# A decoder layer's feed-forward part split into two passes, with a seven-product down projection

## The chip, the cores and the metric

The kernel runs on one core of a Trainium2 chip. TensorE multiplies, VectorE (DVE in the profile) and ScalarE (ACT) do the element-wise work, GpSimd (POOL) does sums over partitions, and nearly all transfers are issued from the queue of SyncE (SP). Times are device microseconds of a whole execution; before and after are compared by the median of several runs. In the profile "PE" is a matmul, "PEld" the load of its stationary operand, and L88 means line 88 of the kernel.

## The reference

The layer takes x, 8 sequences of 100 tokens of width 1024, and a context. It applies a retention-like attention, a cross attention to the context, and a gated feed-forward part, each followed by a residual sum and a normalization without weights. Only the last of the three changes here:

```python
gate = jnp.einsum('bsd,hd->bsh', x, w_gate)      # 4096 x 1024
up = jnp.einsum('bsd,hd->bsh', x, w_up)          # 4096 x 1024
gated = jax.nn.silu(gate) * up
y = jnp.einsum('bsh,dh->bsd', gated, w_down)     # 1024 x 4096
x = _layernorm(x + y, axis=-1)
```

## The kernel before

Everything lies with the model's width on the 128 partitions and tokens along the free dimension. The 800 tokens are two halves of N = 400. The width 1024 is KT = 8 blocks of 128, or two groups of QT = 4. A float32 product is made from three faster ones: each operand is split into a rounded high part and a remainder (`split`, `split2`: a ScalarE cast, L69, and a VectorE subtraction, L70), and `mm3` (L87 to L90) issues high x high, high x low and low x high into one PSUM bank. So one 128 x 128 x 400 block costs three matmuls of 400 columns.

The feed-forward part begins at L761. Its input, the normalized result of the cross attention, is kept as four block operands: b11 and b21 are the upper and lower 512 rows of the first half of the tokens, b12 and b22 those of the second. The hidden width 4096 is 32 blocks of 128, taken in 16 units (`UNITS`) of two.

Gate and up of unit 0 are made directly (L871 to L879): 2 x 2 x 2 products of 8 blocks. For the other 15 units, the function `seven` (L831) treats two hidden blocks x two token halves as a 2 x 2 block matrix product and makes it with 7 block products in place of 8. A block product is `prod`: 4 blocks of contraction x 3 matmuls, 12 matmuls into a bank of its own (`next_bank`). Their sums are made afterwards on VectorE, in the helpers `copied` (ScalarE, L849) and `add` (L853). Mixed weights come from `w_pair` (L814), mixed inputs from `mix_all` (L795), which runs while the direct products of unit 0 and the first products of unit 1 do.

The down projection is not made by seven products. `hidden` (L894) multiplies silu(gate) by up, splits the result and leaves it in on-chip tiles `hd`. Whenever two units are ready (three at the very end), `down` (L911) loads their down weights, and `into_y2` (L905) makes each of the 8 output blocks x 2 token halves and adds it to the on-chip sum `y2`, which starts as the residual. So gate, up and down alternate. The last three units are made over 500 and then 300 tokens (`CUT`); the normalization of the 500 runs under the matmuls of the 300, and that of the 300 (`norm_root`, `scaled`) is the tail.

A second form of the seven-product scheme stands in the first attention: `wino` (L334) with `in_turn` (L390). It keeps three banks per unit and lets TensorE itself add up products in one of them (`start=False`), so that only three VectorE additions and three ScalarE copies are left. `in_turn` interleaves two neighbouring units: one unit's last three products alternate with the first three of the next.

What order instructions have on each engine is settled when the program is built: a scheduler places them by program order (earlier or `high_priority` code first) and by its own model of when each is ready, and gives tiles of a pool their buffers, `bufs` of them to a tag. On the chip each queue then runs strictly in that order. The SP queue in particular holds every load and store: an instruction at its head that waits for a buffer holds back all later transfers.

Raw weights arrive in three buffers `wst` of 512 KB, split weights lie in four buffers `w`, and the `big` pool has four tiles of 1.6 MB.

Of the kernel before, what the change touches and what calls it, by code (L numbers as in the profile page):

```python
# [16 lines left out]
P = 128  # L17
# [17 lines left out]
LAST = 3  # L35
CUT = 5 * T
# [5 lines left out]
def decoder_layer(ctx, tc, xT, cT, w1, wo1, w2, wo2, wc, w3, wd, gw, qw, kw, trig, dec, mask, out):  # L42
# [118 lines left out]
    wcd = dr.tile([2 * NKV, P, 2, KT * P], FR, name="wcd")  # L161

    bigpool = sbuf("big", 2 * KT // QT)
    bp = bigpool.__enter__()
# [159 lines left out]
    def load_raw(src):  # L324
        st = wp.tile([P, KT * P], F32, tag="wst", name="wst", bufs=3)
        nc.sync.dma_start(out=st, in_=src)
        return st
# [6 lines left out]
    def wino(pool, src0, src1, zb, temp, tags):  # L334
# [12 lines left out]
        def copied(acc):  # L347
            t = temp()
            with tc.high_priority():
                nc.scalar.copy(t, acc)  # L350
            return t

        def add(t, acc):
            with tc.high_priority():
                nc.vector.tensor_tensor(t, acc, t, ALU.add)
            return t
# [9 lines left out]
        p1 = copied(x)  # L366
# [4 lines left out]
        c11 = add(p1, z)  # L371
# [3 lines left out]
        u2 = copied(x)  # L375
        yield
        prod(y, (tb, 0), "t3")
        p7 = copied(y)
# [3 lines left out]
        c22 = add(p7, x)  # L382
        yield
        prod(y, (tb, 1), "t4", start=False)
        c21 = add(u2, y)
        yield
        prod(x, (tv, 1), "b22", start=False)
        return c11, x, c21, c22

    def in_turn(units):  # L390

        at = sorted((7 * i + 2 * j, i) for i in range(len(units)) for j in range(-1, 7))
        started = {}
        for _, i in at:
            make, then = units[i]
            if i not in started:
                started[i] = make()
            try:
                next(started[i])
            except StopIteration as e:  # L400
                then(e.value)


    with sbuf("l1", 2) as p:
# [118 lines left out]
        def after_qk(h):  # L523
            def then(c):
                c11, c12, c21, c22 = c
                for (half, i), acc in zip(HB, (c11, c22, c21, c12)):
                    of_qk(half, i, acc)
            return then

        def after_v(h):  # L530
            def then(c):
                c11, c12, c21, c22 = c
                for (half, blk), acc in zip(HB, (c11, c22, c21, c12)):
                    of_v(half, blk, acc, acc is c12)
                core(h)
            return then

        def after_g(h):
            def then(c):
                c11, c12, c21, c22 = c  # L540
                gated(h, {(half, blk): silu(acc, None if acc is c12 else acc)
                          for (half, blk), acc in zip(HB, (c11, c22, c21, c12))})
            return then

        in_turn([(lambda h=h, i=i: wino(p, w1[h, i], w1[h, i + 1], zb, temp, "ass"), then(h))
                 for h in range(1, NH1) for i, then in ((0, after_qk), (2, after_v), (4, after_g))])
# [213 lines left out]

    fp = ctx.enter_context(sbuf("fp", 1, "right"))  # L761
    z2pool = sbuf("z2", 1, "right")
    z2p = z2pool.__enter__()
    zb, ys = {}, []

    def z_tile(name):
        return z2p.tile([P, 2, QT, N], FR, tag=name, name=name)

    def temp(bufs=8):
        return fp.tile([P, N], F32, tag="s", name="s", bufs=bufs)  # L770

    zz = fp.tile([P, 2, 2, QT, N], FR, tag="y2", name="zz")

    def make_z2(half):
        if half == 0:
            return [z_tile("b11"), zz[:, 0]]
        return [zz[:, 1], z_tile("b22")]

    def mix(dst, pairs):
        for j, (a, b, op) in enumerate(pairs):  # L780
            if not isinstance(a, bass.AP):
                rs = y2p.tile([P, N], F32, tag="rs", name="rs", bufs=2)
                nc.sync.dma_start(out=rs, in_=zd2[0, :, a])
                a = rs
            t = y2p.tile([P, N], F32, tag="mix", name="mix")
            nc.vector.tensor_tensor(t, a, b, op)
            split(dst[:, :, j], t)

    def after2(half, y):
        ys.append(y)  # L790
        if half == 0:
            zb["b21-b11"] = z_tile("b21-b11")
            mix(zb["b21-b11"], [(y[:, QT + j], y[:, j], ALU.subtract) for j in range(QT)])

    def mix_all(y):  # L795
        js = range(QT)
        for name, pairs in (("b11+b22", [(j, y[:, QT + j], ALU.add) for j in js]),
                            ("b12-b22", [(y[:, j], y[:, QT + j], ALU.subtract) for j in js]),
                            ("b21+b22", [(QT + j, y[:, QT + j], ALU.add) for j in js]),
                            ("b11+b12", [(j, y[:, j], ALU.add) for j in js])):  # L800
            zb[name] = big([P, 2, QT, N])
            mix(zb[name], pairs)
# [3 lines left out]
    zb["b11"], zb["b22"] = z2[0][0], z2[1][1]  # L806

    ring = [0]

    def next_bank():  # L810
        ring[0] += 1
        return bank("aaassssv"[ring[0] % 8])[:, :N]

    def w_pair(*ops):  # L814

        w = wp.tile([P, 2, KT * P], FR, tag="w", name="w", bufs=4)
        for c, (x, y, op, keep) in enumerate(ops):
            t = x
            if y is not None:
                t = fp.tile([P, H], F32, tag="as", name="as") if keep else x  # L820
                nc.vector.tensor_tensor(t, x, y, op)
            e = slice(c * H, (c + 1) * H)
            split2(w[:, 0, e], w[:, 1, e], t)
        return w

    def first_pair(i, part, r1=None):
        r1 = load_raw(w3[i + 1, part]) if r1 is None else r1
        a21, a22 = r1[:, :H], r1[:, H:]
        return w_pair((a21, a22, ALU.add, True), (a22, None, None, True))

    def seven(i, part, t0=None):  # L831

        r0, r1 = load_raw(w3[i, part]), load_raw(w3[i + 1, part])
        a11, a12, a21, a22 = r0[:, :H], r0[:, H:], r1[:, :H], r1[:, H:]
        t0 = first_pair(i, part, r1) if t0 is None else t0
        t1 = w_pair((a11, a22, ALU.add, True), (a11, None, None, True))
        t2 = w_pair((a12, a22, ALU.subtract, True), (a21, a11, ALU.subtract, False))
        t3 = w_pair((a11, a12, ALU.add, False))

        def prod(w, c, z):  # L840
            acc = next_bank()
            for k in range(QT):
                e = slice(c * H + k * P, c * H + (k + 1) * P)
                mm3(acc, w[:, 0, e], w[:, 1, e], zb[z][:, 0, k], zb[z][:, 1, k], k == 0, k == QT - 1)
            return acc

        def copied(acc):
            t = temp()
            nc.scalar.copy(t, acc)  # L849
            return t  # L850

        def add(t, x, y, op=ALU.add):
            nc.vector.tensor_tensor(t, x, y, op)  # L853

        s2 = copied(prod(t0, 0, "b11"))
        s4 = copied(prod(t0, 1, "b21-b11"))
        add(s2, s2, s4)
        s1 = copied(prod(t1, 0, "b11+b22"))
        add(s1, s1, s4)
        add(s4, s1, s2, ALU.subtract)  # L860
        s3 = copied(prod(t1, 1, "b12-b22"))
        add(s4, s4, s3)
        add(s1, s1, prod(t2, 0, "b21+b22"))
        add(s4, s4, prod(t2, 1, "b11+b12"))
        m5 = prod(t3, 0, "b22")
        add(s1, s1, m5, ALU.subtract)
        add(s3, s3, m5)
        return s1, s3, s2, s4


    ws = [[load_w(w3[i, part]) for part in range(2)] for i in range(2)]  # L871
    gs = []
    for half in range(2):
        for i in range(2):
# [4 lines left out]
            gs.append(t)  # L879
    t0s = [first_pair(2, part) for part in range(2)]  # L880
    mix_all(ys[1])
    y2pool.__exit__(None, None, None)

    with sbuf("ff", 1) as p:
        def new_hid():
            return [p.tile([P, 2, 2 * N], FR, tag="hd", name="hd", bufs=4) for _ in range(2)]

        def gate(i, t0=None):
            g = seven(i, 0, t0)
            for t in g:  # L890
                nc.scalar.activation(t, t, AF.Silu)
            return g

        def hidden(i, g, t0=None, make=new_hid):  # L894
            u = seven(i, 1, t0)
            hid = make()
            for n, (a, b) in enumerate(zip(g, u)):
                nc.vector.tensor_tensor(a, a, b, ALU.mult)
                split(hid[n // 2][:, :, n % 2 * N:(n % 2 + 1) * N], a)
            return hid  # L900

        def load_wd(u, mq, w=None):
            return load_w(wd[u, mq], w)

        def into_y2(ws, hid, m, a, e):  # L905
            acc = bank(acc_tag())[:, :e - a]
            for k, h in enumerate(hid):
                mmw(acc, ws[k // 2], m % QT * 2 + k % 2, h[:, 0, a:e], h[:, 1, a:e], k == 0, k == len(hid) - 1)
# [120 lines left out]
```

## Time and profile before

| what | value |
| --- | --- |
| median of 3 runs (lowest to highest) | 2551.64 us (2550.22 to 2552.69) |
| the profiled execution's own time | 2551.76 us |
| its span, first to last instruction | 2550.0 us |
| matmul instructions recorded | 14186 |
| transfers | 353.93 MB, mean 139 GB/s |

The profiled execution lies within the spread of the timed runs. The page gives busy times of each engine over the span, then 40 slices of 63.75 us each; the feed-forward part begins a little after 1735 us and takes slices 28 to 40. A row of a stretch of time gives for each engine its busy us and its instruction count, then the clock that TensorE was granted (1.00 is full speed), the mean busy share of the 16 DMA engines and the rate. A row of a group of instructions gives line, engine, operation, output and inputs, shape, count, busy us, mean ns of one, then the idle time just before them and what ended it.

### The profile page before, as it was taken

To read this page: it belongs to the slowest core of one execution; us is meant where nothing else is said; L and a number is where in the kernel's file an instruction comes from. 1 tells how busy PE (TensorE), PEld (TensorE's weight loads), DVE (VectorE), ACT (ScalarE), POOL (GpSimd) and SP (SyncE) were. 2 spreads that over 40 slices of the span, in tenths; PEclk is the share of its full clock that TensorE was granted. 3 is DMA by queue.
4 is the path that set the end of the run, shared out by engine and by line. 5 is a ranking of instruction groups with operands and counts; after the bars stand their busy time and mean duration, and the time that the engine had idled before them with its cause. 6 is when DMAs were issued, how large, how long until landed. Compare 5 with 4: busy or idle time off the path is not lost.

```text
span 2550.0 us, 37518 instructions
## 1 busy us (share of the span) xinstructions
PE 2504.3 (98%) x14186; PEld 2462.7 (97%) x14186; DVE 2006.9 (79%) x3316; ACT 1338.8 (53%) x2390; POOL 471.7 (18%) x230
## 2 busy tenths in 40 slices
PE   8999999998999999999999999999999999999997
PEld 8999999998899999999999999999999999999996
DVE  7778876569999788898998998767875865865886
ACT  6676676336777466565565565434432433432351
POOL 0111111002555243333343343100000000000000
PEclk9999999999999999999999999999999999999999
DMA  7333445764444555455455455474412211211221
GB/s 237 109 113 122 142 142 197 246 248 151 140 141 166 185 185 167 132 180 161 145 176 161 150 185 187 139 263 132 141 50 67 83 50 67 83 50 67 67 75 52
DMA packets 165940, 353.93 MB, mean 139 GB/s; under 512 B 45530, under 2 KB 108378, under 8 KB 156542
## 3 DMA queue, kind: packets, MB, share of 16 engines
q1 hardware_dynamic: 164606, 347.33, 40.9%
q0 software_dynamic: 1152, 4.19, 1.1%
q8 instruction: 111, 1.82, 0.3%
q14 instruction: 71, 0.58, 0.1%
HBM read 283.09 MB, written 68.39 MB: 138 GB/s over the span
## 4 chain that ended last, share of the span: by engine, by line
PE 87%; DVE 7%; DMA 2%; issue 2%; ACT 1%; SPq 0%; DVEq 0%; ACTq 0%
PE a L90 16%; PE a L88 16%; PE a L89 16%; PE s L89 10%; PE s L90 10%; PE s L88 10%; PE v L88 3%; PE v L90 2%; PE v L89 2%; DVE r L122 1%; PE s L473 1%; PE s L668 1%; DVE r L121 1%; DVE d L70 1%; DVE w L70 1%
## 5 line engine op out<-in xcount | busy, mean ns | idle before, releaser
L88 PE MATMUL a<-big,w 128*128 128x400 f32 (+2 forms) x1796 | 606.0, 338 | 9.7 <-ACT big L69 6.4
L89 PE MATMUL a<-big,w 128*128 128x400 f32 (+2 forms) x1796 | 606.1, 338 | 0.0
L90 PE MATMUL a<-big,w 128*128 128x400 f32 (+2 forms) x1796 | 604.3, 337 | 0.0
L69 ACT CAST w<-wst 128x1024 fp32r<-128x1024 f32 (+2 forms) x292 | 251.4, 864 | 260.4 <-PE a L90 112.0
L70 DVE TENSOR_TENSOR w<-wst,w 128x1024 fp32r<-128x1024 f32 (+2 forms) x292 | 290.7, 998 | 104.6 <-ACT w L69 103.3
L88 PEld LDWEIGHTS a<-big,w 128*128 128x128 f32 x1796 | 338.4, 188 | 10.9 <-ACT big L69 7.0
L89 PEld LDWEIGHTS a<-big,w 128*128 128x128 f32 x1796 | 338.7, 189 | 1.6 <-DVE big L70 0.6
L90 PEld LDWEIGHTS a<-big,w 128*128 128x128 f32 x1796 | 338.7, 189 | 0.7
L127 POOL PARTITION_ALL_REDUCE ss<-sq x56 | 161.2, 2885 | 332.7 <-DMA zd<-y 166.6
L88 PE MATMUL s<-big,w 128*128 128x400 f32 x596 | 207.9, 350 | 2.4 <-ACT big L69 2.4
L89 PE MATMUL s<-big,w 128*128 128x400 f32 x596 | 206.8, 347 | 1.7 <-DVE big L70 1.7
L90 PE MATMUL s<-big,w 128*128 128x400 f32 x596 | 206.3, 347 | 0.0
L591 POOL PARTITION_ALL_REDUCE kss<-ksq x64 | 165.5, 2586 | 140.8 <-ACT ksq L590 140.1
L69 ACT CAST w<-as 128x512 fp32r<-128x512 f32 x90 | 55.9, 621 | 214.2 <-PE a L90 180.1
L702 ACT ACTIVATE s<-s,rk 128x400 f32<-128x400 f32 x160 | 88.2, 592 | 95.1 <-DVE sm L724 64.5
L127 POOL PARTITION_ALL_REDUCE mb<-sm x32 | 83.4, 2607 | 217.5 <-DVE sm L724 217.5
L853 DVE TENSOR_TENSOR s<-s 128x400 f32<-128x400 f32 x183 | 102.3, 568 | 24.9 <-ACT s L849 19.2
L721 ACT ACTIVATE s<-s 128x800 f32<-128x800 f32 (+1 forms) x128 | 95.3, 749 | 45.6 <-DVE s L715 42.2
L88 PEld LDWEIGHTS s<-big,w 128*128 128x128 f32 x596 | 112.6, 189 | 4.5 <-ACT big L69 3.6
L89 PEld LDWEIGHTS s<-big,w 128*128 128x128 f32 x596 | 112.5, 189 | 3.2 <-DVE big L70 2.3
L90 PEld LDWEIGHTS s<-big,w 128*128 128x128 f32 x596 | 113.0, 190 | 0.0
L70 DVE TENSOR_TENSOR pl<-s,ph 128x800 fp32r<-128x800 f32 (+1 forms) x128 | 108.2, 850 | 1.1 <-ACT ph L69 1.0
(315 smaller groups left out, 6222.6 us busy)
## 6 DMA issues: line engine op xcount, KB each, us to landing
wst<-in_w SPq DMA_DIRECT2D x137, 512.0 KB
w<-wcd SPq DMA_DIRECT2D x64, 1024.0 KB
wst<-in_wo SPq DMA_DIRECT2D x64, 512.0 KB
wst<-in_wd SPq DMA_DIRECT2D x32, 512.0 KB
big<-o1d SPq DMA_DIRECT2D x16, 800.0 KB
qd<-d SPq DMA_DIRECT2D x32, 400.0 KB
q<-qd SPq DMA_DIRECT2D x32, 400.0 KB
o2d<-oh SPq DMA_DIRECT2D x32, 400.0 KB
```

The lines of the kernel that those rows point to most:

```text
L69: nc.scalar.copy(hi, src)
L70: nc.vector.tensor_tensor(lo, src, f32(hi), ALU.subtract)
L88: nc.tensor.matmul(acc, lh, rh, start=start, stop=False, skip_group_check=chain)
L89: nc.tensor.matmul(acc, lh, rl, start=False, stop=False, skip_group_check=chain)
L90: nc.tensor.matmul(acc, ll, rh, start=False, stop=stop, skip_group_check=chain)
L121: nc.vector.scalar_tensor_tensor(q, ss, eps, q, ALU.add, ALU.mult)
L122: nc.vector.scalar_tensor_tensor(q, q, 3.0, r, ALU.subtract, ALU.mult)
L127: nc.gpsimd.partition_all_reduce(y, x, P, op)
L591: nc.gpsimd.partition_all_reduce(ss[:, at], sq[:, at], P, RED.add)
L702: nc.scalar.activation(sc, sp, AF.Copy, scale=rk[:, c:c + 1])
L721: nc.scalar.activation(e, e, AF.Exp)
L853: nc.vector.tensor_tensor(t, x, y, op)
```

## The change

Three parts. First, `wino` becomes the common helper `seven` (raw weights may come as two strided slices; a result is passed to a callback `got`, or added to an existing tile `into`), and the old `seven`, `w_pair`, `first_pair`, `next_bank` and `mix_all` go. Gate and up of units 1 to 15 use the new helper under `in_turn`; the mixed inputs t1 to t4 are made in `after2`, ahead of unit 0's direct products.

Second, gate and up are finished for all units before the down projection begins. `gated_block` multiplies, and `combine` writes each unit's hidden blocks to DRAM: for the first twelve units in the seven forms that the scheme needs as its right operand (`hd`, by quarters of four units, 7 chunks of 1.6 MB to a quarter), for the last four as they are (`h3d`).

Third, the down projection runs as a second pass: for three quarters of the hidden width, `down_unit` makes two output blocks x two token halves by seven block products, added into `y2`; the fourth quarter is made by plain products, half by half of 400 tokens, followed by the normalization. Chunks are loaded one quarter ahead into buffers that the first pass has left (`slots`).

```diff
-    def wino(pool, src0, src1, zb, temp, tags):
+    def seven(pool, src0, src1, zb, tags, temp=None, got=None, into=None):
...
-        def copied(acc):
-            t = temp()
+        def first(acc, name):
             with tc.high_priority():
+                if into is not None:
+                    nc.vector.tensor_tensor(into[name], acc, into[name], ALU.add)
+                    return None
+                t = temp()
                 nc.scalar.copy(t, acc)
...
+        def put(name, j, a, b):
+            t = y2p.tile([P, N], F32, tag="mix", name="mix", bufs=3)
+            nc.vector.tensor_tensor(t, a, b, ALU.subtract)
+            split(zb[name][:, :, j], t)
+            return t
+        for j in range(QT):
+            r = []
+            for k in (j, QT + j):
+                r.append(y2p.tile([P, N], F32, tag="rs", name="rs", bufs=2))
+                nc.sync.dma_start(out=r[-1], in_=zd2[0, :, k])
+            t2 = put("t2", j, y[:, QT + j], put("t1", j, y[:, j], r[0]))
+            put("t3", j, y[:, QT + j], y[:, j])
+            put("t4", j, r[1], t2)
...
+    def gated_block(u, name, acc):
+        if u not in hid:
+            hid[u] = ff.tile([P, 4, N], F32, tag="r", name="r")
+        r = hid[u]
+        at = r[:, C.index(name)]
...
+            nc.vector.tensor_tensor(at, acc, gates[u, name], ALU.mult)
+        done[u] = done.get(u, 0) + 1
+        if done[u] == 4:
+            combine(u, r)
+    def combine(u, r):
+        h = ff.tile([P, 7, N], FR, tag="h", name="h")
+        q, j = u // QT, u % QT
+        if q == QT - 1:
+            split2(h[:, 0:4], r, r)
...
+            return
+        t = ff.tile([P, 4, N], F32, tag="t", name="t")
+        pairs = r.rearrange("p (i x) n -> p i x n", x=2)
+        nc.vector.tensor_tensor(t[:, 0:2], pairs[:, :, 1], r[:, 0:2], ALU.subtract)
+        nc.vector.tensor_tensor(t[:, 2], r[:, 3], t[:, 0], ALU.subtract)
+        nc.vector.tensor_tensor(t[:, 3], r[:, 2], t[:, 2], ALU.subtract)
+        split2(h[:, 3:7], t, t)
+        split2(h[:, 1:3], r[:, 2:4], r[:, 2:4])
+        split2(h[:, 0], r[:, 0], r[:, 0])
+        to = lambda a, b, l: f32(hd[q, a:b, :, l, j]).rearrange("c p n -> p c n")
+        nc.sync.dma_start(out=to(0, 7, 0), in_=f32(h))
+        nc.sync.dma_start(out=to(0, 1, 1), in_=r[:, 0:1])
+        nc.sync.dma_start(out=to(1, 3, 1), in_=r[:, 2:4])
+        nc.sync.dma_start(out=to(3, 7, 1), in_=t)
...
+    def after_up(u):
+        if u == QT:
+            load_chunk(0, down_order[:1])
+        elif u == UNITS - 2:
+            load_y(fp)
+        elif u == UNITS - 1:
...
+            load_y(ctx.enter_context(sbuf("yy", 1)))
+            slots[0:0] = [lambda: hk.tile([P, 2, QT, N], FR, tag="h", name="h", bufs=2)] * 2
+    slots = [f_tile, z_tile, z_tile] + [lambda: big([P, 2, QT, N])] * 4 + [z_tile]
+    down_order = ("b11", "b21", "t2", "t3", "t1", "t4", "b22")
...
+    def load_chunk(q, names):
+        for name in names:
+            chunk[q, name] = next_slot()
+            nc.sync.dma_start(out=f32(chunk[q, name]), in_=f32(hd[q, ORDER7.index(name)]))
...
+    def down_unit(q, m):
+        def make():
+            if m == 0 and q == 0:
+                load_chunk(0, down_order[1:])
+            z = {name: chunk[q, name] for name in ORDER7}
+            into = {"c%d%d" % (i + 1, j + 1): y2[m // 2][:, i, j * N:(j + 1) * N] for i in range(2) for j in range(2)}
+            return seven(fp, down_w(q, m), down_w(q, m + 1), z, "ass", into=into)
+        def then():
+            if m != 2:
+                return
+            if q < QT - 2:
+                load_chunk(q + 1, down_order)
+            else:
+                for half in range(2):
+                    z3.append([next_slot() for _ in range(2)])
+                    for i in range(2):
+                        nc.sync.dma_start(out=f32(z3[half][i]), in_=f32(h3d[2 * i + half]))
+        return make, then
...
+    in_turn([unit(u) for u in range(1, UNITS) for unit in (gate_unit, up_unit)]
+            + [down_unit(q, m) for q in range(QT - 1) for m in range(0, KT, 2)])
...
-            for a, e in ((0, CUT), (CUT, 2 * N)):
...
+            y = rows(half)
+            s1 = lnp.tile([P, N], F32, tag="s1", name="s1", bufs=2)
+            for m in range(KT):
+                acc = proj(w_split(load_raw(down_w(QT - 1, m))), z3[half], tag=acc_tag())
+                nc.vector.tensor_tensor(y[:, m], y[:, m], acc, ALU.add)
+                add_up(s1, y, m)
+            r = norm_root(y, s1, lnp, idle_pe=half == 1)
+            scaled(y, r, lambda m, half=half: out[:, m, half * N:(half + 1) * N])
```

`down_w` slices the down weights so that each transfer moves runs of 128 values (512 bytes).

## The prediction

> **What bounds the kernel now.** First the busy shares, then TensorE's waits, then stretches of the feed-forward part.
>
> ```profile
> span 2550.0 us, 37518 instructions
> PE 2504.3 (98%) x14186; PEld 2462.7 (97%) x14186; DVE 2006.9 (79%) x3316; ACT 1338.8 (53%) x2390; POOL 471.7 (18%) x230
> PE a L88 <- ACT big L69: 6.4, 1, 6.4
> 100.00:400.00 300.00, 299.81 (x1802) 297.73 (x1801) 230.05 (x339) 207.83 (x330) 38.18 (x18) 1.00 0.41 130
> 1664.00:1684.00 20.00, 18.72 (x99) 18.09 (x99) 13.65 (x21) 8.01 (x12) 0.00 (x0) 1.00 1.03 404
> 1735.00:1818.00 83.00, 78.33 (x399) 75.02 (x400) 65.39 (x119) 38.78 (x72) 0.00 (x0) 0.96 0.45 147
> 1800.00:1850.00 50.00, 45.93 (x233) 44.13 (x232) 39.47 (x71) 21.46 (x40) 0.00 (x0) 0.93 0.32 101
> 1850.00:2450.00 600.00, 600.00 (x3294) 599.92 (x3293) 427.96 (x739) 216.75 (x403) 0.00 (x0) 1.00 0.20 65
> 2530.40:2550.00 19.60, 6.70 (x20) 2.77 (x19) 14.22 (x30) 7.68 (x16) 0.00 (x0) 0.82 0.47 168
> ```
>
> TensorE is the bound, and from 1850 to 2450 it never pauses at full clock: 3294 matmuls in 600 us are 182.2 ns each, the price of a 400-column matmul here. DVE has room (71%), transfers far more (65 GB/s; 1664 to 1684 shows that 404 can be had, all DMA engines busy). The losses of the feed-forward part lie at its ends. From 1735 to 1818, 399 matmuls ran where 83 / 0.1822 = 456 fit: 57 x 0.182 = 10 us lost, of which the largest single wait of the whole list, 6.4 us for a `big` tile (a mixed input), is one. After the last product at 2530.4 come 19.6 us of normalization. The first attention (100 to 400 us) runs `wino` and `in_turn` already: TensorE gapless there with DVE at 230 / 300 = 77%.
>
> **Matmuls removed.** Direct products of unit 0 and the seven-product gate and up stay: 192 + 15 x 2 x 84 matmuls. Down before: 32 hidden blocks x 8 output blocks x 2 halves x 3 = 1536. After: three quarters x 4 units x 84 = 1008, and the last quarter 8 x 8 x 2 x 3 = 384; together 1392. So 144 fewer; at 182.2 ns from the 1850 to 2450 row **-26.2 us**. The 500- and 300-column split goes too, but it counted the same columns, so it adds nothing. All of it is on the path, since TensorE has no pause to hide it in. This is the firm term.
>
> **Does anything else become the bound in pass one?** The unit of work is gate plus up, 168 x 0.1822 = 30.6 us of TensorE. The DVE rows of the two forms:
>
> ```profile
> L70 DVE TENSOR_TENSOR w<-wst,w 128x1024 fp32r<-128x1024 f32 x48 | 58.5, 1220 | 45.2 <-ACT w L69 45.2
> L355 DVE TENSOR_TENSOR tp<-s,tp 128x400 f32<-128x400 f32 x33 | 18.8, 569 | 13.8 <-PE s L90 11.6 <-ACT w L69 2.1
> L363 DVE TENSOR_TENSOR ws<-wst 128x512 f32<-128x512 f32 x16 | 11.0, 689 | 0.3
> L853 DVE TENSOR_TENSOR s<-s 128x400 f32<-128x400 f32 x117 | 65.6, 568 | 13.0 <-ACT s L849 9.8 <-PE s L90 2.8
> L821 DVE TENSOR_TENSOR as<-wst 128x512 f32<-128x512 f32 x62 | 42.5, 685 | 26.1 <-DMA wst<-in_w 26.1
> ```
>
> The old `seven` took 9 additions x 0.568 + 5 weight sums x 0.685 + 7 remainders x 0.685 = 13.3 us of DVE. The new takes 4 x 0.69 + 3 x 1.22 + 0.69 + 3 x 0.569 = 8.8. Two of them, 4 products silu(gate) x up (2.3) and `combine` (1600 elements of differences and 2800 of remainders, eleven times the 400-column 0.569, less the overhead saved on wide ones: an estimate of 5.4 us) make 25.3 us of 30.6: 83%, somewhat above the 77% that left TensorE gapless. ACT needs about 14. So pass one should stay TensorE-bound: **0**, up to +15 if it doesn't (third rival). `combine` also stores 2.87 MB a unit; with 2.1 MB of weights 163 GB/s against 404. It hides.
>
> **Start of the feed-forward part.** `mix_all` and `b21-b11` mixed 20 tiles, `after2` mixes 16, and weight sums of the first unit shrink. The old wait arose because mixing was put behind the next units' weights. Now mixing stands ahead. From the end of the normalized rows (1765 us in DVE's order of time) DVE has 8 remainders of z (8 x 0.49, back to back), 14 mixes until t2 is whole (14 x 0.98), first unit's weights 5.9 and odd ends 1.5: ready near 1790, less up to 4 us of weight work that fits the pauses before. TensorE wants t2 after the direct products and two block products, near 1782 + 4.4 = 1787. So a wait of 0 to 4 us where 10 were lost: -10 to +5 against now, taken as **-4**.
>
> **The junction of the passes.** Here the new cost lies. `load_chunk` needs the buffers of z and `big` that the last up unit is still reading, so six chunks (6 x 1.64 = 9.8 MB) can only be fetched as that unit's products release them. With the weights of two or three down units (2.1 to 3.1), the stores of units 14 and 15 (3.3) and y2 (3.3), 18.5 to 19.5 MB want to move within 19 block products, 19 x 12 x 0.1822 = 41.5 us. At the measured 404 GB/s that takes 46 to 48 us, 5 to 7 late; part of it (unit 15's store, half of y2) isn't needed at once, which takes off up to 8 us of traffic. The Trainium skill's "DMA: Bandwidth & Descriptors", Bandwidth, speaks against the change more: for traffic between HBM and on-chip memory it gives a limit of about 358 GB/s per core. By it the junction would be 10 to 13 us late. The trace of this kernel shows 404 for 20 us, so I go by the row: 0 to 7, taken as **+5**; by the page's figure it would be +11. A wait of that length costs more than itself: the 1800 to 1850 stretch, after the 6.4 us wait, shows a mean clock of 0.93. The skill's "TensorE: Matmul & The Clock Gate" (Part 1) puts this at half clock after an idle window of about 3.4 us; 7% of 50 us is 3.5 us, which I let stand in the +5 and in the wide side of the range.
>
> **Pass two.** A down unit takes 84 x 0.1822 = 15.3 us; DVE 7.1 + 7 additions x 0.569 = 11.1 (73%), now for every bank, since `first` with `into` leaves ScalarE. A quarter (61 us) loads 11.5 MB of chunks and 4.2 of weights, 257 GB/s of 404. The weights come in 512-byte runs, which the trace doesn't show; packets under 2 KB are most of its packets all the same. Bounds: nothing, or half the weights' rate (+13 us of transfers a quarter, still under 61). Chunks are asked for ten products before they are used, 22 us. The price is what `then` puts on SP ahead of the next weights: three chunks with free buffers, 4.9 MB, 12 us, against about five products (11 us) for which three `wst` buffers let weights run ahead. **+2** over three boundaries, 0 to 30 (second rival).
>
> **The tail.** 400 columns for 300: eight subtractions (+0.8), sixteen variance matmuls (5.2 us in the tail, +1.1), the chain of roots (+0.5), the scaling (+0.8), the last store (+0.3); less 0.7, since the other part's scaling no longer sits between, as its half is done under the last 192 matmuls (35 us, DVE some 31 of them). **+2.5**, 0 to +5.
>
> **Sum** against the profiled execution's own 2551.8: -26.2 - 4 + 5 + 2 + 2.5 = -20.7, so 2531.1. That execution is 0.1 us above the median of the runs, so the same figure stands for the median: **2531 us**.
>
> **Rivals.** First, *the junction hides and the start loses nothing*: -26.2 - 9 + 2.5 gives 2519. For it: 404 GB/s, and old chunks known long before; against it: the six buffers come free only one by one. Chance 0.16.
>
> Second, *weights queue behind chunks on SP*, the case slower than before. At the junction and the two quarter boundaries after it, SP's one queue carries chunk transfers ahead of weights. Four chunks are 16.2 us at 404 GB/s, a unit's weights 2.6, their split 1.05 + 1.22; 21 us against a lead of 11 leaves TensorE idle for 10, three times, 30 us more: 2561. It decides from (2551.8 - 2531.1) / 3 = 7 us a boundary. For it: a queue in strict order, and `load_chunk` ahead of a unit's weights in the program; against it: the scheduler places a load only when its model has the buffer free, and 257 of 404 GB/s is no saturation on the mean. Chance 0.11.
>
> Third, *pass one becomes bound by DVE*: the tile `r` is single, so the next unit's first product of silu(gate) and up waits until `combine` has been stored. From the last block product of a unit to that one lie 4 products, 8.7 us; multiply, differences, cast, remainder and a 1.43 MB store (3.5 us at 404, plus its latency) need about 12. DVE then stands at a wait for some 3 us of its 5 spare a unit. If 1.3 us of each reaches TensorE, 15 x 1.3 = 20 us are lost: 2551, no change. Chance 0.08.
>
> **How the numbers follow.** The main course has 0.65; its own range is 2523 to 2543 (junction +11, start +1, or both small). Its gain alone is firm, its stalls are not. The range 2517 to 2555 takes in the first rival but its edge, the third, and part of the second. The measurement tells 0.2%, 5.1 us, from no change. Faster: 0.65 + 0.16 + a third of the third rival = 0.84; same 0.05; slower 0.11.
>
> **What would show it.** Right: 14042 matmuls or so; rows of pass one and of pass two at full clock with 5.49 matmuls a us, DVE near 80% and 70%; a DMA share near 1 for some 40 us at the junction, and TensorE's waits there on chunk loads or weights, 2 to 10 us in all; the wait for `big` at the start under 5 us; a tail near 22 us. Wrong: waits for `wst` or `w` at each quarter boundary, or DVE waits for stores of `r` that reach TensorE, or a pass one under 5.4 matmuls a us.

## The result and the profile after

| | before | after |
| --- | --- | --- |
| median of 5 runs each, us | 2552.58 (2550.22 to 2555.21) | 2527.52 (2526.38 to 2527.76) |
| the profiled execution's own time / its span, us | 2551.76 / 2550.0 | 2527.58 / 2525.8 |
| feed-forward part: first matmul to last product, us from the span's start | 1735.1 to 2530.3 | 1735.7 to 2504.6 |
| matmuls recorded | 14186 | 14042 |
| transfers, MB | 353.93 | 438.16 |

The ratio is 0.9901 with a 95% interval of 0.9887 to 0.9916: faster by 1%. By the two profiled spans it is 24.2 us. The prediction said 2531 us, 20.7 us less than before. The total is near; three of its terms (the start, the junction and pass two) are not, and they partly cancel.

First the head of the page after: its span, TensorE's row (busy us, share, count), and the row of the DMA engines' busy tenths in 40 slices of 63 us.

```profile
span 2525.8 us, 37215 instructions
PE 2478.2 (98%) x14042; PEld 2440.9 (97%) x14042; DVE 2000.6 (79%) x3106; ACT 1353.7 (54%) x2272; POOL 466.8 (18%) x230
...
DMA  7333445774444654455554554575455445388742
```

TensorE lost 26.1 us of busy time. The slices 3, 8, 8, 7 near the end (2147 to 2400 us) are the place where one pass gives way to the other.

Now the stretches of the feed-forward part after. The columns are from:to, length, busy us and count of PE, PEld, DVE, ACT, POOL, the granted clock, the DMA engines' busy share, GB/s.

```profile
1735.70:1818.00 82.30, 82.25 (x443) 80.88 (x444) 73.48 (x126) 42.82 (x72) 0.00 (x0) 1.00 0.43 137
1818.00:2220.00 402.00, 402.00 (x2208) 402.00 (x2207) 312.54 (x413) 194.34 (x271) 0.00 (x0) 1.00 0.47 161
2220.00:2260.00 40.00, 40.00 (x222) 40.00 (x221) 28.15 (x38) 14.08 (x19) 0.00 (x0) 1.00 1.00 372
2260.00:2300.00 40.00, 38.95 (x209) 37.41 (x208) 23.97 (x35) 8.20 (x9) 0.00 (x0) 1.00 0.91 322
2300.00:2350.00 50.00, 46.50 (x246) 45.63 (x245) 33.93 (x50) 11.44 (x13) 0.00 (x0) 0.97 0.67 239
2350.00:2500.00 150.00, 150.00 (x821) 149.41 (x821) 93.55 (x136) 41.31 (x47) 0.00 (x0) 1.00 0.51 169
2504.60:2525.80 21.20, 7.40 (x19) 2.75 (x18) 10.27 (x20) 6.43 (x12) 0.00 (x0) 0.79 0.21 77
```

Read it by counts: 5.49 matmuls a us is a TensorE that never pauses. The first stretch has 443 of 452 that fit; before, 399 of 456. Pass one, 1818 to 2220, is without a gap. The junction (2220 to 2260) has the DMA engines full and no pause at all. The next two stretches are where time goes: 209 of 219.5, and 246 of 274.5. After 2350 it is dense again to the end of the products.

Adding up how much later than 0.182 us after its predecessor each matmul starts (excesses under 0.05 us left out), within those stretches, gives the ledger that the rest of this text uses. Such a sum is good to some 0.2 us.

| term | us | how read |
| --- | --- | --- |
| 144 matmuls fewer | -26.2 | 14186 - 14042, at 182.2 ns |
| start of the feed-forward part | -8.7 | pauses and slow matmuls: 10.5 before, 1.8 after |
| junction | 0 | 222 matmuls in 40 us |
| pass two | +7.8 | two stalls, about 2291 and 2328 |
| slow matmuls in the last quarter | +0.9 | at 2473 and 2494, beside the first half's normalization |
| tail | +1.5 | 19.7 to 21.2 |
| part ahead, not changed | +0.7 | starts at 1735.1 and 1735.7 |
| sum | -24.0 | spans: -24.2 |

The second stall is the larger one, 5.6 us. SyncE's queue in order of time (start, us from the first issue's start to the last one's end, what, how many; `wst` are down weights, the rest chunks of later quarters), then what DVE, ScalarE and TensorE did; a bracket is the idle time before an instruction and what ended it, and no bracket means that it followed at once. L364 adds a product to the sum `y`, L370 is the first sum made of the new weights.

```profile
2302.81 0.34 SPq L911 DMA_DIRECT2D z<-hd  x1
2305.36 2.51 SPq L911 DMA_DIRECT2D big<-hd  x2
2308.05 8.02 SPq L327 DMA_DIRECT2D wst<-in_wd  x4
2316.16 2.37 SPq L911 DMA_DIRECT2D big<-hd  x1
```

```profile
2320.77 0.57 DVE L364 TENSOR_TENSOR y<-s,y 128x400 f32<-128x400 f32 x1 [0.52 <-PE s L88]
2322.96 0.58 DVE L364 TENSOR_TENSOR y<-s,y 128x400 f32<-128x400 f32 x1 [1.62 <-PE s L88]
2325.15 0.57 DVE L364 TENSOR_TENSOR y<-a,y 128x400 f32<-128x400 f32 x1 [1.61 <-PE a L88]
2325.64 0.68 DVE L370 TENSOR_TENSOR ws<-wst 128x512 f32<-128x512 f32 x1
```

```profile
2327.20 1.99 ACT L67 CAST w<-wst 128x1024 fp32r<-128x1024 f32 x2 [18.18 <-DVE wst L371]
```

```profile
2328.30 0.45 PE L86 MATMUL s<-f,w 128*128 128x400 f32 x1 [3.19 <-ACT w L67]
...
2329.75 0.54 PE L87 MATMUL a<-h,w 128*128 128x400 f32 x1
```

And the DMA engines' busy tenths from 2300 to 2330, in 40 slices of 0.75 us:

```profile
DMA  9997988999999999999999989999999992000000
```

Three chunk loads, 4.9 MB, were issued just ahead of the four pieces of down weights that TensorE needs next; the two to `big` are for the third quarter, which TensorE reaches some 50 us later. The issuing of the four pieces took 8.0 us, where a single one at 2299.7 took 0.43. The last thing that keeps the engines full, until 2325, is the chunk asked for at 2316.2.

But the weights were not late for all of the time until 2325.6. The semaphores in the trace show the two pieces that L370 needs landed at 2319.6 and 2320.5, 12 us after they were asked for, and the other two by 2322.1. L370 began 5.2 us after the second of its pieces was there, and its row has no idle time before it: it stood in VectorE's own order behind three additions, each of which waited for a product of TensorE. From L370's start to the waiting matmul's start takes 2.7 us; begun at 2320.5 it would, by an estimate from these figures, have let that matmul go at 2323.2, and TensorE's pause began at 2325.1. So what held TensorE last was VectorE's order, which is settled when the program is built. At the first stall it was the same: the weights had landed at 2286.2, and the additions kept their first sum until 2290.9.

ScalarE had been idle 18.2 us; TensorE stood 3.2 us for the cast, and then ran a few us at half speed (matmuls of 0.54 us for 0.34).

### The profile page after: what moved, and what is told of

It is laid out like the page before. It is cut to its first block, busy times and chain, and to the rows that moved or that the text cites. A ratio compares the mean times of both kernels' runs of the same rounds, so it can differ in the third digit from the quotient of the medians.

```text
span 2525.8 us, 37215 instructions
## 1 busy us (share of the span) xinstructions
PE 2478.2 (98%) x14042; PEld 2440.9 (97%) x14042; DVE 2000.6 (79%) x3106; ACT 1353.7 (54%) x2272; POOL 466.8 (18%) x230
## 2 busy tenths in 40 slices
DMA packets 232898, 438.16 MB, mean 173 GB/s; under 512 B 47594, under 2 KB 176490, under 8 KB 220302
## 4 chain that ended last, share of the span: by engine, by line
PE 89%; DVE 6%; issue 2%; DMA 1%; ACT 1%; SPq 0%; DVEq 0%; ACTq 0%
PE a L88 18%; PE a L86 18%; PE a L87 17%; PE s L88 9%; PE s L87 9%; PE s L86 9%; PE v L86 2%; PE v L88 2%; PE v L87 2%; PE s L486 1%; PE s L677 1%; DVE r L120 1%; DVE r L119 1%; PE s L148 1%; DVE d L68 1%
## 5 line engine op out<-in xcount | busy, mean ns | idle before, releaser
L86 PE MATMUL a<-big,w 128*128 128x400 f32 (+2 forms) x1824 | 616.3, 339 | 10.5 <-ACT big L67 7.1
L87 PE MATMUL a<-big,w 128*128 128x400 f32 (+2 forms) x1824 | 615.7, 338 | 0.0
L88 PE MATMUL a<-big,w 128*128 128x400 f32 (+2 forms) x1824 | 614.4, 338 | 0.0
L67 ACT CAST w<-wst 128x1024 fp32r<-128x1024 f32 (+1 forms) x243 | 251.8, 1039 | 431.0 <-PE s L88 152.3
L68 DVE TENSOR_TENSOR w<-wst,w 128x1024 fp32r<-128x1024 f32 (+1 forms) x243 | 297.7, 1227 | 120.2 <-ACT w L67 119.0
L86 PEld LDWEIGHTS a<-big,w 128*128 128x128 f32 x1824 | 343.7, 189 | 12.3 <-ACT big L67 7.4
L87 PEld LDWEIGHTS a<-big,w 128*128 128x128 f32 x1824 | 344.5, 189 | 1.4 <-DVE big L68 0.3
L88 PEld LDWEIGHTS a<-big,w 128*128 128x128 f32 x1824 | 344.2, 189 | 1.0 <-DVE w L68 0.3
L86 PE MATMUL s<-big,w 128*128 128x400 f32 x680 | 236.0, 347 | 0.1
L87 PE MATMUL s<-big,w 128*128 128x400 f32 x680 | 234.7, 345 | 0.0
L88 PE MATMUL s<-big,w 128*128 128x400 f32 x680 | 234.6, 346 | 0.0
L86 PE MATMUL a<-z,w 128*128 128x400 f32 x504 | 174.5, 346 | 8.2 <-ACT r L118 4.3
L88 PE MATMUL a<-z,w 128*128 128x400 f32 x504 | 174.9, 347 | 0.7 <-DVE w L68 0.7
L87 PE MATMUL a<-z,w 128*128 128x400 f32 x504 | 175.0, 347 | 0.0
L87 PE MATMUL s<-z,w 128*128 128x400 f32 x416 | 144.5, 347 | 2.3 <-DVE z L68 2.3
L86 PE MATMUL s<-z,w 128*128 128x400 f32 x416 | 145.2, 349 | 0.0
L88 PE MATMUL s<-z,w 128*128 128x400 f32 x416 | 145.1, 349 | 0.0
L86 PEld LDWEIGHTS s<-big,w 128*128 128x128 f32 x680 | 127.6, 188 | 1.4 <-ACT w L67 0.4
L87 PEld LDWEIGHTS s<-big,w 128*128 128x128 f32 x680 | 127.6, 188 | 1.1
```

The lines of the kernel that those rows point to most:

```text
L67: nc.scalar.copy(hi, src)
L68: nc.vector.tensor_tensor(lo, src, f32(hi), ALU.subtract)
L86: nc.tensor.matmul(acc, lh, rh, start=start, stop=False, skip_group_check=chain)
L87: nc.tensor.matmul(acc, lh, rl, start=False, stop=False, skip_group_check=chain)
L88: nc.tensor.matmul(acc, ll, rh, start=False, stop=stop, skip_group_check=chain)
```

## Experiments

Three batches of kernels, each compared with the kernel before on the same chip; times are medians.

### How much is the count of matmuls worth?

All four quarters of the down projection are made by plain products again, from h3d; two passes, gate and up by the new helper and everything ahead are kept. The first form fetched three of the first quarter's four chunks only when the first pass had ended:

```diff
-    hd = dr.tile([QT - 1, 7, P, 2, QT, N], FR, name="hd")
-    h3d = dr.tile([4, P, 2, QT, N], FR, name="h3d")
+    h3d = dr.tile([QT, 4, P, 2, QT, N], FR, name="h3d")
...
+    in_turn([unit(u) for u in range(1, UNITS) for unit in (gate_unit, up_unit)])
+    load_chunk(0, ("c21", "c12", "c22"))
+    for q in range(QT - 1):
+        z = [[chunk[q, "c1%d" % n], chunk[q, "c2%d" % n]] for n in (1, 2)]
+        for m in range(KT):
+            if m == 2:
+                load_chunk(q + 1, ("c11", "c21", "c12", "c22"))
+            w = w_split(load_raw(down_w(q, m)))
+            for half in range(2):
+                acc = proj(w, z[half], tag=acc_tag())
+                nc.vector.tensor_tensor(y[:, m], y[:, m], acc, ALU.add)
```

> Both passes kept, gate and up as changed, but all four quarters of the down projection by plain products: 144 matmuls come back (1536 for 1392), combine only splits and stores 1.64 MB a unit, a quarter loads 6.5 MB for 11.5. If the matmul count is the gain: 2527.5 + 144 x 0.1822 = 2553.7, less up to 7.1 us of waits in pass two that the smaller transfers may end, so 2547 to 2554. If the two-pass form or the regrouped gate and up is the gain: within 5 us of 2527.5.

Measured: 2578.72 us, ratio 1.0108 (1.0093 to 1.0123), slower than before. TensorE's waits (instruction, what it waited for: us in all, times, longest):

```profile
PE s L86 <- DMA h<-h3d: 30.1, 1, 30.1
```

This run added a wait of its own: two chunks were put into buffers that only come free when the last pool of pass one closes, and were loaded in one go. It says nothing about the count of matmuls; it does show what a bare junction costs, 30 us, when its chunks are not spread out.

The second form loads the three chunks at the last up unit, into buffers free by then:

```diff
         elif u == UNITS - 1:
+            load_chunk(0, ("c21", "c12", "c22"))
             ffpool.__exit__(None, None, None)
...
-            slots[0:0] = [lambda: hk.tile([P, 2, QT, N], FR, tag="h", name="h", bufs=2)] * 2
+            slots[4:4] = [lambda: hk.tile([P, 2, QT, N], FR, tag="h", name="h", bufs=2)] * 2
```

> As plain_down, but the first quarter's hidden blocks are fetched into buffers that come free before the last unit's end (z and big for the two tiles over the pools just closed), so that the junction's wait of 30 us, this variant's own, is gone. If the matmul count is the gain: 2547 to 2554, that is 20 to 26 us over the changed kernel. If plain_down's 2578.7 was slow for another reason than that wait: 2565 or more.

Measured: 2546.10 us, ratio 0.9976 (0.9968 to 0.9983): 6.2 us below the kernel before. Junction and the start of pass two in this kernel:

```profile
2220.00:2260.00 40.00, 40.00 (x222) 40.00 (x221) 19.01 (x23) 11.58 (x16) 0.00 (x0) 1.00 1.01 378
2260.00:2350.00 90.00, 90.00 (x495) 90.00 (x494) 24.74 (x31) 11.59 (x11) 0.00 (x0) 1.00 0.67 224
```

It has the old 14186 matmuls and no stall. It is 18.6 us above the changed kernel; 26.2 for the matmuls less the 7.8 of stalls that it doesn't have is 18.4. So the term for the matmuls is worth what it was said to be, and two passes alone, with the better start, make up the 6.2 us. The form with four chunks a quarter also moves 29.5 MB less, so it can't say which transfers make the stalls.

### Are the chunks of the next quarter what makes the stalls?

First by leaving work out: chunks of the second and third quarter are not loaded, the first quarter's stand in.

```diff
             if q < QT - 2:
-                load_chunk(q + 1, down_order)
+                for name in down_order:
+                    chunk[q + 1, name] = chunk[q, name]
```

> The chunks of quarters 1 and 2 are not loaded, those of quarter 0 are used again (this leaves that part of the computation out, all instructions of TensorE, VectorE and ScalarE stay). If chunk transfers queued ahead of weights cost the 7.1 us lost in pass two: 2520.5. If 512-byte weight runs or VectorE's part cost them: 2525 or more.

Measured: 2528.23 us, ratio 0.9911 (0.9896 to 0.9925): no gain. The profiled execution took 2531.49 us, the longest of this kernel's four. By the sum over matmul starts its pauses of pass two fell only from 7.8 to 5.8. Where they stand:

```profile
2262.70:2302.70 40.00, 37.54 (x192) 36.71 (x191) 23.14 (x33) 8.19 (x9) 0.00 (x0) 0.93 0.73 250
```

That would speak against the chunks, but SyncE's queue shows that the last quarter's operands had moved up into the space that was left: two loads of `h` and one of `z` from h3d, 4.9 MB, at 2269.6 to 2270.6. One transfer was traded for another, and the tail was longer too (24.6 us). As a test of the transfers it is inconclusive.

So the same bytes were kept and their place in the queue was changed. The next quarter's chunks must be issued behind the newest down weights:

```diff
+    last_w = [None]
     def load_raw(src):
...
-                nc.sync.dma_start(out=st[:, i * H:(i + 1) * H].rearrange("p (u c) -> p u c", u=QT), in_=s)
+                last_w[0] = nc.sync.dma_start(out=st[:, i * H:(i + 1) * H].rearrange("p (u c) -> p u c", u=QT), in_=s)
...
             if m != 2:
                 return
-            if q < QT - 2:
-                load_chunk(q + 1, down_order)
-            else:
+            with tc.issue_after(last_w[0].ins):
+                if q < QT - 2:
+                    load_chunk(q + 1, down_order)
+                else:
```

> Loads of the next quarter's chunks are made to stand in SP's queue behind the newest down weights, those of the unit after the one that asks for them; same bytes, same work. If the 7.8 us of waits in pass two come from chunks that are fetched well before they are used and so delay weights that are used soon: the second wait (5.6 us) falls to 1 or less, the whole is 2520 to 2523. If the bytes are simply too many for the time: 2526 to 2529.

Measured: 2521.62 us, ratio 0.9883 (0.9867 to 0.9900). The second stall is gone; the first, 2.5 us, is still there. Asked for one unit of two output blocks later:

```diff
-            if m != 2:
+            if m != 4:
```

> As paced, one unit later (chunks asked for after the third of a quarter's four units). If too early chunks are the cause, both waits shrink: 2519 to 2522. If they now come too late for the next quarter's first product, TensorE waits for chunks instead: 2527 or more.

Measured: 2518.68 us, ratio 0.9870 (0.9856 to 0.9885), the fastest of all, 8.8 us below the changed kernel (8.0 if the gains over the kernel before, each measured beside it, are compared). Its stretches and its queue (the row of ten spans 28.6 us because it holds waits for free buffers too):

```profile
2220.00:2260.00 40.00, 40.00 (x221) 40.00 (x220) 27.75 (x37) 13.97 (x18) 0.00 (x0) 1.00 1.03 374
2260.00:2300.00 40.00, 40.00 (x222) 39.99 (x221) 24.83 (x37) 7.55 (x9) 0.00 (x0) 1.00 0.93 316
2300.00:2350.00 50.00, 50.00 (x276) 50.00 (x275) 35.86 (x52) 12.51 (x14) 0.00 (x0) 1.00 0.71 254
```

```profile
2292.85 2.54 SPq L913 DMA_DIRECT2D z<-hd  x2
2295.60 0.32 SPq L913 DMA_DIRECT2D big<-hd  x1
2303.03 28.62 SPq L329 DMA_DIRECT2D wst<-in_wd  x10
2331.74 1.40 SPq L913 DMA_DIRECT2D big<-hd  x3
```

The stretches of pass two have all their matmuls, at a DMA share of 0.93 and 0.71 against 0.91 and 0.67. Ten pieces of weights now go out before three more chunks do. The engines are as full as before. Of the 8.8 us, 7.7 are the pauses (10.5 in the whole part after, 2.8 here); most of the rest is that this execution came to the feed-forward part 1.0 us earlier.

That a later request for chunks removes the stalls is shown. By which way is not, for the edit moved two things: the transfers, and VectorE's order with them. In this kernel the first weight sum follows its weights at once; those of the sixth unit of pass two landed at 2313.8 (L357 and L372 are the L355 and L370 of the changed kernel):

```profile
2313.45 0.57 DVE L357 TENSOR_TENSOR y<-a,y 128x400 f32<-128x400 f32 x1 [1.25 <-PE a L88]
2313.95 0.69 DVE L372 TENSOR_TENSOR ws<-wst 128x512 f32<-128x512 f32 x1
```

### Is it the one queue, or the short runs?

Two other explanations for late weights: that they stand behind the chunks in SyncE's queue, so another queue would help, and that runs of 512 bytes are slow. Down weights relaid so that each row is one run of 4096 bytes:

```diff
-        w = wd[q * QT:(q + 1) * QT, m // QT].rearrange("u p c -> p u c")
-        c = m % QT * 2 * P
-        return [w[:, :, c + i * P:c + (i + 1) * P] for i in range(2)]
+        return wd[q, m]
```

> Down weights laid out so that one transfer of 4096-byte runs brings what two of 512-byte runs brought; same bytes, same matmuls. If the short runs cause the waits of pass two: 2520.5. If the order behind the chunks does: the weights still queue[...], 2525 to 2526. If neither counts: 2527.5.

Measured: 2528.13 us, ratio 0.9913 (0.9896 to 0.9929). The stalls are 2.2 and 6.0 us, with the same wait of 3.2 us for the cast of a weight. The length of the runs isn't the cause: the weights landed 7.9 and 6.1 us before VectorE's first sum of them.

Down weights issued from ScalarE's queue, the layout as in the change:

```diff
-                nc.sync.dma_start(out=st[:, i * H:(i + 1) * H].rearrange("p (u c) -> p u c", u=QT), in_=s)
+                nc.scalar.dma_start(out=st[:, i * H:(i + 1) * H].rearrange("p (u c) -> p u c", u=QT), in_=s)
```

> The down weights of pass two are issued from ScalarE's queue instead of SP's. If weights were late because they stood behind bulk transfers in SP's queue: most of the 7.8 us lost there is gone, 2520 to 2523. If the transfers together were too many for the engines: 2526 to 2529, as the bytes are the same.

Measured: 2539.66 us, ratio 0.9950 (0.9936 to 0.9965): 12.1 us slower than the changed kernel. TensorE's wait for weights in this whole run, then ScalarE and its queue:

```profile
PE a L86 <- ACT w L67: 9.0, 8, 3.9
```

```profile
2237.20 7.42 ACTq L327 DMA_DIRECT2D wst<-in_wd  x4
...
2313.85 11.51 ACTq L327 DMA_DIRECT2D wst<-in_wd  x2
...
2371.18 17.09 ACTq L327 DMA_DIRECT2D wst<-in_wd  x4
2388.36 1.04 ACT L67 CAST w<-wst 128x1024 fp32r<-128x1024 f32 x1 [18.42 <-issue]
```

```profile
2389.46 0.62 PE L86 MATMUL a<-big,w 128*128 128x400 f32 x1 [3.89 <-ACT w L67]
```

With the DMA engines full (share 1.01 both from 2220 to 2260 and from 2370 to 2388), the issues on ScalarE took 7.4, 11.5 and 17.1 us, and casts stand behind them on the same engine: the one at 2388.36 began as soon as the last issue was over, its weights had landed at 2366 and been summed by 2370, and TensorE stood 3.9 us for it. That place is a third stall, 6.5 us, which the changed kernel doesn't have. A second queue doesn't bring weights past transfers that already fill the engines either: those asked for at 2312.7 took 16 us to land.

Both together:

```diff
-            nc.sync.dma_start(out=st, in_=src)
+            (nc.scalar if act else nc.sync).dma_start(out=st, in_=src)
...
+        return wd[q, m]
```

> w_act and w_contig together, and the last quarter's weights from ScalarE's queue too. If the queue is the cause: 2519 to 2522, not slower than w_act. If ScalarE's issues hold back its casts: over 2527.

Measured: 2527.11 us, ratio 0.9906 (0.9891 to 0.9921). The loss of the run before is gone, probably because one piece of weights in place of two leaves ScalarE free more often, but stalls of 3.1 and 5.0 us stay. Neither the queue nor the runs, nor both, removes them. Yet here the weights for the second stall landed at 2317.3, 3 us sooner than in the changed kernel. They lay there for 6.4 us:

```profile
2323.22 0.57 DVE L364 TENSOR_TENSOR y<-s,y 128x400 f32<-128x400 f32 x1
2323.70 0.68 DVE L370 TENSOR_TENSOR ws<-wst 128x512 f32<-128x512 f32 x1
```

Counting along VectorE's order in each trace shows what these kernels have in common. Pass two makes 12 down units, 7 additions into `y` each; the stalls come with the weights of the fourth and the sixth. How many additions stand ahead of the first weight sum of each, how long its weights had been there by then, and the stall (the first from 2260 to about 2300, the second from there to about 2350), in us:

| kernel | fourth: additions | weights there for | stall | sixth: additions | weights there for | stall |
| --- | --- | --- | --- | --- | --- | --- |
| changed kernel | 22 | 4.7 | 2.2 | 37 | 5.2 | 5.6 |
| w_contig | 22 | 7.9 | 2.2 | 37 | 6.1 | 6.0 |
| w_contig_act | 22 | 6.6 | 3.1 | 36 | 6.4 | 5.0 |
| w_act | 22 | 7.8 | 4.5 | 37 | 0.8 | 5.6 |
| reuse_chunks | 22 | 4.3 | 5.8 | 28 | 1.2 | 0 |
| paced | 22 | 5.2 | 2.5 | 32 | 0.5 | 0 |
| paced4 | 16 | 0.2 | 0 | 33 | 0.1 | 0 |

At these two places there is a stall wherever the count is 22, or 36 to 37, and none where it is lower. In all but one of the cases with a stall the weights had been there for 4 us or more. So weights that are there sooner don't help while the count stays. What part the landing has beside it stays open: in the kernels without a stall the weights had also landed sooner (the sixth's at 2312.7 to 2313.8, against 2317.3 to 2329.5), and no run kept the transfers and moved the sums alone. Why moving the chunks moves the weight sums is argued only: the scheduler orders VectorE by its own model of when weights arrive.

### What made the start of the feed-forward part faster?

Two edits of the kernel before. In the first, the load of y2 (3.3 MB), which stands in the queue amid the row loads for mixing, must wait for the last of those:

```diff
+        with tc.issue_after(last_rs[0].ins):
             for half in range(2):
                 nc.sync.dma_start(out=y2[:, :, half * N:(half + 1) * N], in_=zd2[half])
```

> The kernel before, its residual load y2 (two transfers of 1.6 MB) made to wait in the SP queue until the last row for the mixed inputs is asked for. If the start's 10 us were lost because rows and weights lay behind these transfers: 7 us gained or more, 2545 or less against 2552. If VectorE's mixing work itself was too long: no change, 2552.

In the second, two of the four mixed inputs of `mix_all` are left out and the other two stand in for them:

```diff
-                            ("b12-b22", [(y[:, j], y[:, QT + j], ALU.subtract) for j in js]),
-                            ("b21+b22", [(QT + j, y[:, QT + j], ALU.add) for j in js]),
-                            ("b11+b12", [(j, y[:, j], ALU.add) for j in js])):
+                            ("b12-b22", [(y[:, j], y[:, QT + j], ALU.subtract) for j in js])):
...
+        zb["b21+b22"], zb["b11+b12"] = zb["b11+b22"], zb["b12-b22"]
```

> The kernel before, with two of the four late mixed inputs left out (8 of 20 mixed tiles and 8 of their rows; the other two stand in, so that part of the result is another). If making the mixed inputs in time was the start's loss: its 7.9 us after the first 40 us fall to 2 or less, 2544 to 2546. If weights of the units were what came late: 2550 or more.

Measured: y2_late 2548.85 us, ratio 0.9989 (0.9980 to 0.9997); half_mix 2544.78 us, ratio 0.9973 (0.9963 to 0.9982). The stretch in each, y2_late first:

```profile
1735.00:1818.00 83.00, 79.32 (x413) 76.57 (x414) 68.56 (x125) 41.74 (x77) 0.00 (x0) 0.98 0.45 140
```

```profile
1735.00:1818.00 83.00, 81.92 (x440) 80.42 (x441) 70.65 (x130) 43.08 (x80) 0.00 (x0) 1.00 0.42 138
```

Of the 7.9 us that the kernel before loses around 1802 to 1812, holding back y2's load saves 2.7, and halving the mixed inputs saves all. So the loss was mixed inputs not ready in time, and y2's load a third of that. The changed kernel has both remedies: it loads y2 hundreds of us later and mixes 16 tiles for 20. How much each has in its own gain, and whether it also gains by making the mixed inputs in another order, was not separated.

## Why the prediction was right or wrong

**Matmuls removed, -26.2: right.** 14042 were recorded, as said, at the same 182 ns; the run with plain products returned the amount.

**Pass one bound by TensorE, 0: right.** DVE is busy 312.5 of 402 us, 78%, where 83% was estimated. The wait that the third rival rested on exists and is too short to matter. DVE's groups and its wait in pass one:

```profile
L68 DVE TENSOR_TENSOR w<-wst,w 128x1024 fp32r<-128x1024 f32 x53 | 64.9, 1224 | 16.3 <-ACT w L67 15.3
...
L68 DVE TENSOR_TENSOR t<-t,h 128x1600 f32<-128x1600 f32 x11 | 20.1, 1825 | 0.9
```

```profile
DVE r L843 <- DMA hd<-r: 3.8, 5, 1.4
```

The wait for stores of `r` came to 3.8 us in five times over the whole pass, where the rival took some 3 us a unit, and none of it reached TensorE.

**Start, -4: right in sign, half in size (-8.7), and wrong in its reading.** The step named the 6.4 us wait for a `big` tile as one of the losses at the start of the feed-forward part. That row came from the list over the whole span. It lies in the first 10 us of the execution, and the kernel after has it there too (6.7 us). TensorE's waits of before in 1735 to 1818 alone, then the stretch behind them:

```profile
PE s L88 <- ACT big L69: 2.4, 3, 1.0
PE s L89 <- DVE big L70: 1.7, 1, 1.7
```

```profile
1806.00:1812.00 6.00, 5.51 (x15) 4.66 (x16) 4.70 (x9) 2.11 (x5) 0.00 (x0) 0.50 0.38 102
```

The true loss was several short waits one after another, nearly all for mixed inputs, then 6 us at half clock with more such waits in it, so 15 matmuls ran where 33 fit. The clock of 0.93 that the prediction tied to the 6.4 us wait belongs to these. And the reason for a remaining wait, 14 mixes before t2 is whole, was too dear: only 1.8 us of pauses are left, most of them in the first 40 us. The prediction's own working, a wait of 0 to 4 us where 10 were lost, comes to -10 to -6; the -4 that it took does not follow from it. Nor is there a pause as long as the 3.4 us that it named for the half clock: the longest one ahead of it was 1.7 us.

**Junction, +5: wrong, it is 0, the lower end of its own range of 0 to 7.** The traffic was as foreseen: the DMA engines are full, share 1.00. What failed is the step that wanted 18.5 to 19.5 MB moved "within 19 block products". In the 40 us from 2220 only 372 GB/s x 40 us = 14.9 MB moved, and 12.9 more in the 40 us after; TensorE didn't need it sooner. The chunk b11 had been loaded at 1896, and in TensorE's timeline block products on it alternate with products on other tiles, from 2235.7 on. That work on it, drawn forward, is what covers the junction is argued from the timeline; no run took it away. The 358 GB/s of the Trainium skill ("DMA: Bandwidth & Descriptors", Bandwidth) isn't a limit in this trace: 372 over 40 us here, mixed with stores. The term that was made from it, +11, fails for the same reason as the +5.

**Pass two, +2: mis-sized, it is +7.8, and the last step of the wait was not foreseen.** Both the +2 and the second rival had chunks standing ahead of weights, with 12 us of transfers against a lead of 11. That much happened: the weights for the second stall took 12 us to land. The rival had the price at three places and 10 us each; it was 2.2 and 5.6 us, both in the 80 us after the junction. What neither had is VectorE's order: at both stalls the weights had landed 4.7 and 5.2 us before their first sum, which stood behind additions that wait for products. (0.8 us of the first stall is TensorE waiting for such an addition to free a bank.) The argument against the rival, that a load is placed only when its buffer is free, didn't help: the `big` buffers were free early, so loads were placed long before anybody read them. And 257 of 404 GB/s was a mean over a quarter; in the first 40 us of the pass the engines were 91% busy, with y2 and four chunks of the second quarter besides the weights. The remedy that the rival would suggest, another queue for the weights, does harm (w_act); a later request for chunks removes all of it (paced4). The "+13 us" for weights at half rate is a slip: 4.2 MB at 404 GB/s are 10.4 us, so half the rate adds 10; nothing hung on it.

**Tail, +2.5: +1.5.** 21.2 us where "near 22" was said. Its parts add up to 2.8, not 2.5.

The total missed by only 3.5 us because three errors one way (start -4.7, junction -5, tail -1) were partly made up by those the other way (pass two +5.8, 0.9 in the last quarter, 0.7 ahead of the part). That it came so near is luck; the matmuls and the bound of pass one are not.

## What to carry to other kernels

Where a transfer isn't urgent, try tying its issue behind the urgent ones: here asking later for the same bytes turned 25 us of gain into 33. But when an engine waits, look at when its data landed before blaming the transfer. Here the weights had been there for 5 us, and what stood in the way was the order of another engine, settled at build time, which an edit of the loads had moved. A mean rate over a stage says little about its busiest stretch; look at windows of 40 us. And before a wait is booked to a stage, ask the trace for the waits of that stage alone.

## What the runs showed of the hardware

An issue is not always cheap: on SyncE four issues of weights took 8.0 us at one point, 5.9 of them one issue, and on ScalarE two took 11.5 and four 17.1, all while the DMA engines had much to do (share 1.03 from 2308 to 2320 on SyncE's side, 1.01 from 2370 to 2388 on ScalarE's). On SyncE only other transfers stand behind; on ScalarE a cast did, and TensorE behind it.

TensorE fell to half clock without one long pause. Before, matmuls started 1.4, 2.1 and 1.3 us after their predecessors within 5.2 us, with a single matmul at 0.3 us among them, and a stretch at 0.50 followed. After, one matmul that started 3.5 us after its predecessor, at 2328, had the same effect (0.57 from 2329 to 2333), while distances of 0.4 to 1.0 us from 2291 to 2294 had none.
